# An edge-attention stage with its order taken from the source: two steps per chunk, mixing of two tiles at a time, floor and subtraction fused

## The chip, the core and the metric

The kernel runs on one core of one Trainium2 chip. The metric is device time of one execution in microseconds; the time of a kernel is the median of several executions. Engines are named as in the profile: PE (TensorE, with PEld for its weight loads), DVE (VectorE), ACT (ScalarE), POOL (GpSimd) and SP (SyncE). POOL issues the indirect DMAs that gather rows by index, and SP most other DMAs.

## What is computed

Input are 3125 nodes with 512 features and 53,125 edges (25,000 drawn pairs in both directions, and a loop at each node). Cut to its core the reference is

```python
xn = layernorm(x)
# GNN, two layers, 8 heads of 64
h = xn
for l in range(2):
    q, k, v = (h @ Wq[l].T + bq[l]) * 64**-0.5, h @ Wk[l].T, h @ Wv[l].T
    scores = einsum('ehd,ehd->eh', q[tgt], k[srcidx])          # one per edge and head
    p = exp(scores - segment_max(scores, tgt)[tgt])
    w = p / (segment_sum(p, tgt)[tgt] + 1e-16)
    attn = segment_sum(w[:, :, None] * v[srcidx], tgt) @ Wo[l].T + bo[l]
    h = batchnorm(h + attn)
    h = batchnorm(h + relu(h @ W1[l].T + b1[l]) @ W2[l].T + b2[l])
# mixing: linear attention over all nodes
qm, km = softmax(xn @ Wq.T + bq, by head), softmax(xn @ Wk.T + bk, by head)
ctx = km.T @ (xn @ Wv.T + bv)
mix = ((qm @ ctx) / (qm . sum(km)) + qm) @ Wp.T + bp
x = x + layernorm(h) + mix
x = x + mixture_of_8_experts(layernorm(x), top 2)
```

## The kernel before

Nodes are sorted by their number of edges and cut into 25 tiles of 128 (the last has 53). A tile has a fixed number of *slots* (`CAPS`: 44 for tile 0, then 26 down to 10, 453 in all): slot j holds the j-th source node of each of the 128 targets, with a mask where there is none. So one slot of one tile is one gather of 128 rows, each with V and K of a source node (4 KB), from the table `kvd` in HBM.

The program runs in stages: a front stage (layernorm, sorting, keys and values of layer 0), then for each of the two layers the *edge stage* `attention`, then feed-forward and batch norms and, between the layers, the next keys and values; at the end the experts (`last`). The change is in the edge stage.

**Blocks and chunks.** A tile is one block of slots, tile 0 two halves of 22. A block is cut into *chunks* of two slots, 232 per layer. For a chunk, `Block.scores` issues two gathers on POOL (L583), then on DVE the product of K with the query (L588) and its sum by head (L589, the *reduction*). When all scores of a block are there, `Block.exponentials` adds the mask, takes the maximum by head (L600), raises it to a floor of -1e20 (L601), subtracts it (L602) and takes the exponential on ACT (L603). `Block.weights` sums (L611) and divides. While the chunks of the next block are scored, those of this block are weighed: `weigh` multiplies V with the weights, three chunks of five by 16 activations on ACT (L624), the others on DVE (L627). `add_up` then has PE transpose and add the rows up in PSUM (L644, for half blocks L639). `finish` (L678) copies the sum, and after each group of four tiles takes the output projection in four steps: PE into the PSUM tile `po` (L701), DVE adds it to `xg` (L705).

**Lanes and places.** The gathered rows live in lanes, five in layer 0 and four in layer 1. A lane has 5 or 6 places that overlap by half: place p takes V at half p and K at half p+1, so the V of the next place of a lane overwrites the K of this one. Chunks take lanes in turn. So a gather waits for the reduction of the chunk that had the lane before (five chunks back in layer 0, four in layer 1), and, a whole round later, for the add of the chunk 20 back.

**Beside the chunks.** Generators deliver steps of other work, spread evenly over the chunks: in layer 0 `contexts` (5 steps a tile: projections of the transposed normed rows zT, exponentials, PE into the contexts), in layer 1 `mixed` (9 steps a tile, one tile at a time): projection into `pq` (L720, L723), maximum by head on DVE (`hm`, L731), exponentials on ACT (L734), reciprocal (`hr`, L740) and product on DVE (L814), transposes on PE (L454) and a copy on ACT, PE with the contexts (`mpo`, L821), reciprocal and product on DVE (`den`, L829, L830), transposes (L839), a copy, the last projection, a copy and a store. `turned` (L752) loads zT for the next tile on SP.

`places(t)` (L529) prepares tile t: in layer 0 POOL gathers its z rows into the single buffer `part` (L541), PE transposes them (L454) and ACT copies them to `xg`; in layer 1 SP loads `xg`. `query` (L551) makes the tile's q on PE (L555, L557) and ACT (L560).

**What sets the order.** The source gives the instructions in the order of this loop, and a scheduler that works on the whole edge stage decides in which order each engine takes them. Each engine takes its own in that order, and waits at the head of its queue for what an instruction needs.

Of the kernel before, what the change touches and what calls it, by code (L numbers as in the profile page):

```python
# [68 lines left out]

LAYER_COLS = 29  # L70
# [14 lines left out]
def gps_layer(ctx: ExitStack, tc: tile.TileContext, x, src, dst, cols, rows,  # L85
# [21 lines left out]
    kvd = [tc.dram_tile([N, 2 * D], F32, name=f"kvd{l}") for l in range(L)]  # L107
    wqo = [const.tile([128, NP, D], F32, name=name) for name in ("wq", "wo")]
# [280 lines left out]
    with tc.If(flag < 1) as fits:  # L389
        listed_layers(tc, cols=cols, rec=rec, idx=idx, mask=mask, kvd=kvd, zd=zd, ztd=ztd, xb=xb,  # L390
                      base=base, wqo=wqo, layer_weights=layer_weights, **args)
# [18 lines left out]
def listed_layers(ctx: ExitStack, tc: tile.TileContext, rows,  # L410
# [3 lines left out]
                  wqo, layer_weights):  # L414
# [10 lines left out]

    mixb = main.tile([128, L, NP], F32, name="mixb")
    for i, r in enumerate((ROW_BK, ROW_BQ)):
        nc.sync.dma_start(mixb[:, i, :], rows[r].rearrange("(c p) -> p c", p=128))
# [71 lines left out]
    def attention(l, stats, wq, wo, mixw):  # L500
        with tc.tile_pool(name="att", bufs=1, reuse_waits="tile") as ap, \
# [4 lines left out]
            taken_places = [0]  # L506

# [16 lines left out]

            c0 = l * LAYER_COLS + BQ
            bq = bias_rows("bq", colt[:, c0:c0 + NP])
            bm = bias_rows("bm", mixb[:, l, :])

            def places(t):  # L529
# [9 lines left out]
                if not l:  # L539
                    z = ap.tile([P, D], F32, name="part")  # L540
                    nc.gpsimd.indirect_dma_start(  # L541
                        out=z[:n], out_offset=None, in_=zd[:, :],
                        in_offset=bass.IndirectOffsetOnAxis(ap=node(t), axis=0))
                    o = (t - t0) * P
                    to_features(pp, "tr", xg[gi][:, :, o:o + n], z, n, nc.scalar.copy)
# [5 lines left out]
            def query(t):  # L551
# [8 lines left out]
                nc.scalar.activation(q[:n], ps[:n], AF.Copy, scale=float(DH) ** -0.5)  # L560
                return q

            class Block:
# [9 lines left out]
                def scores(self, i):  # L573
# [7 lines left out]
                    for k in range(g):  # L581
# [6 lines left out]
                    nc.vector.tensor_mul(ks, ks, self.q[:n, None, :].to_broadcast([n, g, D]))  # L588
                    nc.vector.tensor_reduce(  # L589
                        self.sc[:n, :, j:j + g].rearrange("p h g -> p g h"),  # L590
                        ks.rearrange("p g (h d) -> p g h d", h=H), AX.X, OP.add)

                def exponentials(self):

                    n, w = self.n, self.w
                    sc = self.sc[:n, :, :w]
                    o = OFFS[self.t] + self.j0
                    nc.vector.tensor_add(sc, sc, mask[:n, None, o:o + w].to_broadcast([n, H, w]))
                    m = ap.tile([P, H], F32, name="m", bufs=3)
                    nc.vector.tensor_reduce(m[:n], sc, AX.X, OP.max)  # L600
                    nc.vector.tensor_scalar(m[:n], m[:n], FLOOR, None, op0=OP.max)  # L601
                    nc.vector.tensor_sub(sc, sc, m[:n, :, None].to_broadcast([n, H, w]))  # L602
                    nc.scalar.activation(sc, sc, AF.Exp)  # L603
                    self.m = m

                def weights(self):

                    n, w = self.n, self.w
                    sc = self.sc[:n, :, :w]
                    s = ap.tile([P, H], F32, name="s", bufs=3)  # L610
                    nc.vector.tensor_reduce(s[:n], sc, AX.X, OP.add)  # L611
                    if self.whole:
                        inverse_sum(s, n)
                        nc.vector.tensor_mul(sc, sc, s[:n, :, None].to_broadcast([n, H, w]))  # L614
                    self.s = s
# [33 lines left out]
            def scaled(o, agg, f, n):  # L649
                for h in range(H):  # L650
                    hs = slice(h * DH, (h + 1) * DH)
                    nc.scalar.activation(o[:n, hs], agg[:n, hs], AF.Copy, scale=f[:n, h:h + 1])

# [4 lines left out]
            def together(a, b, o):  # L658
# [13 lines left out]
                part = ap.tile([P, D], F32, name="part")  # L672
                for k, e, to in ((a, f[0], o), (b, f[1], part)):
                    nc.vector.tensor_mul(e[:n], e[:n], m[:n])
                    scaled(to, k.agg, e, n)
                nc.vector.tensor_add(o[:n], o[:n], part[:n])

            def finish(blocks):  # L678
# [10 lines left out]
                else:  # L689
                    a = ap.tile([P, D], F32, name="a")  # L690
                    together(blocks[0], blocks[1], a)
                    to_features(pp, "tr", at, a, n, nc.scalar.copy)
# [65 lines left out]
            def contexts(t):  # L758

                n = TILES[t][1]  # L760
                if t + 1 < FT:
                    turned(t + 1)
                z = zT.pop(t)
# [5 lines left out]
                ps = project(n, lambda c: z[:, c, :n], wv)  # L769
                yield  # L770
# [14 lines left out]
                elif t == FT // 2:  # L785
                    rowv.append(ap.tile([P, D], F32, name="a"))
# [14 lines left out]
            def mixed(t):  # L801

                n = TILES[t][1]
                if t + 1 < FT:
                    turned(t + 1)
                z = zT.pop(t)
                ps = project(n, lambda c: z[:, c, :n], wmq, bm)
                yield
                q = ap.tile([P, D], F32, name="mq")
                s = exponentials(q, ps, n)  # L810
# [4 lines left out]
                yield  # L815
                qT = ap.tile([128, NP, P], F32, name="mqT")
                to_features(pp, "tr", qT[:, :, :n], q, n, nc.scalar.copy)
# [17 lines left out]
                oT = ap.tile([128, NP, P], F32, name="mqT")  # L835
# [7 lines left out]
                nc.scalar.copy(oT[:, :, :n], ps[:, :NP * n].rearrange("p (c r) -> p c r", c=NP))  # L843
# [3 lines left out]
                y = ap.tile([P, D], F32, name="my")  # L847
# [4 lines left out]
            def beside():  # L852
                for t in range(FT):
                    yield from mixed(t) if l else contexts(t)
# [10 lines left out]
            each = 9 if l else 5  # L865
            steps, done, taken = beside(), 0, 0
            number = FT * each
            chunks = sum((w + G - 1) // G for t, j0, w in todo if t < FT - 2)
            chunks += (todo[0][2] + G - 1) // G

            before, held, ending = None, [], iter(())
            places(0)
            turned(0)
            q = query(0)
            places(1)
            for _ in range(each):
                next(steps)
                taken += 1
            for t, j0, w in todo + [(None, 0, 0)]:
                now, k = None, 0  # L880
                if t is not None:
                    now = Block(t, j0, w, q)
                    k = len(now.chunks)
                kb = len(before.chunks) if before else 0
                for i in range(max(k, kb)):
                    if i < k:
                        now.scores(i)
                        done += 1 if before else 2
                    if i == 0 and before:
                        before.weights()  # L890
                    if i < kb:
                        before.weigh(i)
                    next(ending, None)
                    while (taken - each) * chunks < (number - each) * done and taken < number:
                        next(steps)
                        taken += 1
                    if i < kb:
                        before.add_up(i)
# [825 lines left out]
```

## Time and profile before

| | |
|---|---|
| median of 3 runs | 2837.37 us (2830.23 to 2837.75) |
| the profiled execution | 2804.75 us |
| its span, first to last instruction | 2803.0 us |
| mean granted PE clock | 0.911 |
| edge stage of layer 0, first product to the last output projection | 284 to 1103 us |
| edge stage of layer 1 | 1347 to 2266 us |
| gathers L583 | 906, 1.27 us each on POOL, median 6.3 us from issue to landing |
| products L588 | 464, 1.19 us each on DVE |
| reductions L589 | 464, 1.19 us each on DVE |
| weighing on ACT, L624 | 3888 activations of 0.34 us |
| weighing on DVE, L627 | 214, 1.20 us each |

How to read the lines that follow below. A line of the timeline has start, duration, engine, line of the kernel, operation, output <- inputs, form, count, and in brackets the idle time before it with what the profile thinks ended it. A row of a group has busy time and mean ns of one after the bar. A row of waits names the waiting instruction, the one waited for, then the total in us, the number of waits and the longest. Of several things waited for, the profile names the one whose event came last, and this is inferred.

### The profile page before, as it was taken

To read this page: it belongs to the slowest core of one execution; us is meant where nothing else is said; L and a number is where in the kernel's file an instruction comes from. 1 tells how busy PE (TensorE), PEld (TensorE's weight loads), DVE (VectorE), ACT (ScalarE), POOL (GpSimd) and SP (SyncE) were. 2 spreads that over 40 slices of the span, in tenths; PEclk is the share of its full clock that TensorE was granted. 3 is DMA by queue.
4 is the path that set the end of the run, shared out by engine and by line. 5 is a ranking of instruction groups with operands and counts; after the bars stand their busy time and mean duration, and the time that the engine had idled before them with its cause. 6 is when DMAs were issued, how large, how long until landed. Compare 5 with 4: busy or idle time off the path is not lost. (4 is left out here: it accounts for less than half of the span.)

```text
span 2803.0 us, 30800 instructions
## 1 busy us (share of the span) xinstructions
PE 2398.1 (86%) x8935; PEld 1302.4 (46%) x8935; DVE 2054.1 (73%) x3186; ACT 1406.5 (50%) x5315; POOL 1414.4 (50%) x1153
## 2 busy tenths in 40 slices
PE   6987989889889876999697787979888486999998
PEld 3442445545455543344344555555555344444443
DVE  7810999999999985500679888989988566666663
ACT  1111568787776763200276767776767423222220
POOL 3362778888777770011657766676765323222100
PEclk9998999999999987999798888989999796999999
DMA  8434999999999984321869888989887441111000
GB/s 287 171 121 138 328 331 337 332 330 338 330 326 325 332 266 159 122 108 78 286 234 335 287 299 292 329 303 331 309 307 269 131 135 51 34 48 48 32 19 20
DMA packets 214478, 620.58 MB, mean 221 GB/s; under 512 B 48068, under 2 KB 53569, under 8 KB 210199
## 3 DMA queue, kind: packets, MB, share of 16 engines
q0 software_dynamic: 161696, 518.18, 52.4%
q1 hardware_dynamic: 50048, 95.36, 9.4%
q10 hardware_dynamic: 2556, 4.97, 0.5%
q8 instruction: 75, 1.23, 0.2%
q14 instruction: 103, 0.84, 0.1%
HBM read 543.80 MB, written 74.75 MB: 221 GB/s over the span
## 5 line engine op out<-in xcount | busy, mean ns | idle before, releaser
L583 POOL DMA_INDIRECT lane<-kvd,idx x906 | 1147.7, 1267 | 526.7 <-issue 179.7
L624 ACT ACTIVATE lane<-lane,sc 128x64 f32<-128x64 f32 x3888 | 945.4, 339 | 117.9 <-DVE sc L614 117.6
L588 DVE TENSOR_TENSOR lane<-lane,q 128x1024 f32<-128x1024 f32 (+1 forms) x464 | 549.0, 1193 | 161.8 <-DMA lane<-kvd,idx 146.7
L644 PE MATMUL agg<-ident,lane 128*128 128x128 f32 (+1 forms) x3272 | 531.6, 301 | 140.5 <-DVE lane L627 59.5
L644 PEld LDWEIGHTS agg<-ident,lane 128*128 128x128 f32 (+1 forms) x3272 | 424.2, 154 | 316.1 <-ACT lane L624 143.5
L589 DVE TENSOR_REDUCE sc<-lane 128x16 f32<-128x1024 f32 (+1 forms) x464 | 545.5, 1187 | 2.6 <-ACT lane L624 1.6
L627 DVE TENSOR_TENSOR lane<-lane,sc 128x1024 f32<-128x1024 f32 (+1 forms) x214 | 252.3, 1197 | 0.1
L1089 DVE SCALAR_TENSOR_TENSOR yall<-py,prob,yall 128x512 f32<-128x512 f32 (+1 forms) x200 | 148.8, 748 | 112.4 <-PE py L1087 100.8
L555 PE MATMUL pq<-wq,xg 128*128 128x512 f32 (+1 forms) x400 | 201.7, 634 | 18.5 <-ACT kt L734 12.2
L701 PE MATMUL po<-aT,wo 128*128 128x512 f32 (+1 forms) x448 | 194.2, 572 | 20.3 <-ACT aT L688 13.4
L1087 PE MATMUL py<-w2t,hT 128*128 128x512 f32 (+1 forms) x400 | 188.7, 610 | 1.8 <-ACT hT L1083 0.8
L1080 PE MATMUL ph<-xT,w1t 128*128 128x512 f32 x320 | 156.3, 630 | 0.0
L1095 POOL DMA_INDIRECT out<-yall,rec x25 | 25.0, 1001 | 252.3 <-DVE yall L1089 247.4
L1083 ACT ACTIVATE hT<-ph,colt 128x512 f32<-128x512 f32 (+1 forms) x56 | 35.4, 633 | 211.0 <-PE ph L1080 210.8
L494 POOL DMA_INDIRECT kvd<-kv,rec x25 | 24.7, 989 | 222.8 <-DVE kv L491 216.8
L491 DVE COPY kv<-pv 128x512 f32<-128x512 f32 (+1 forms) x25 | 17.3, 692 | 153.4 <-PE pv L488 153.4
L701 PEld LDWEIGHTS po<-aT,wo 128*128 128x128 f32 x448 | 80.3, 202 | 97.9 <-issue 64.9
L1087 PEld LDWEIGHTS py<-w2t,hT 128*128 128x128 f32 (+1 forms) x400 | 71.9, 189 | 101.3 <-issue 69.0
L555 PEld LDWEIGHTS pq<-wq,xg 128*128 128x128 f32 (+1 forms) x400 | 73.4, 199 | 92.8 <-issue 68.3
L372 ACT COPY kv<-pkv 128x512 f32<-128x512 f32 (+1 forms) x50 | 29.2, 585 | 163.8 <-PE pkv L370 136.4
L1012 POOL DMA_INDIRECT bt<-base,rec x25 | 26.8, 1072 | 160.1 <-DVE yall L1019 150.3
L370 PE MATMUL pkv<-wk,xT 128*128 128x512 f32 (+1 forms) x200 | 100.7, 637 | 5.8 <-ACT kv L372 5.8
(264 smaller groups left out, 3288.4 us busy)
## 6 DMA issues: line engine op xcount, KB each, us to landing
lane<-kvd,idx POOLq DMA_INDIRECT x906, 6.3
kvd<-kv SPq DMA_DIRECT2D x24, 512.0 KB, 2.7
zT<-ztd SPq DMA_DIRECT2D x48, 256.0 KB, 5.3
xmid<-xg SPq DMA_DIRECT2D x10, 1024.0 KB, 5.7
xT<-xmid POOLq DMA_DIRECT2D x10, 1024.0 KB, 10.3
xr<-in_x SPq DMA_DIRECT2D x24, 256.0 KB, 3.9
xb<-xo SPq DMA_DIRECT2D x24, 256.0 KB, 5.6
zd<-z SPq DMA_DIRECT2D x24, 256.0 KB, 2.7
```

The lines of the kernel that those rows point to most:

```text
L370: nc.tensor.matmul(ps[:n], lhsT=xT[t][:, c, :n], rhs=wkv[name][:, c, :], start=(c == 0), stop=(c == NP - 1))
L555: nc.tensor.matmul(ps[:n], lhsT=of_place(t, c), rhs=wq[:, c, :], start=(c == 0), stop=False)
L583: gets.append(nc.gpsimd.indirect_dma_start(out=kv[:n, k, :], out_offset=None, in_=kvd[l][:, :], in_offset=bass.IndirectOffsetOnAxis(ap=idx ...
L588: nc.vector.tensor_mul(ks, ks, self.q[:n, None, :].to_broadcast([n, g, D]))
L589: nc.vector.tensor_reduce(self.sc[:n, :, j:j + g].rearrange("p h g -> p g h"), ks.rearrange("p g (h d) -> p g h d", h=H), AX.X, OP.add)
L624: nc.scalar.activation(v[:, k, h, :], v[:, k, h, :], AF.Copy, scale=self.sc[:n, h, j + k:j + k + 1])
L627: nc.vector.tensor_mul(v, v, self.sc[:n, :, j:j + g].rearrange("p h g -> p g h")[:, :, :, None] .to_broadcast([n, g, H, DH]))
L644: nc.tensor.matmul(self.agg[:, c * n:(c + 1) * n], lhsT=kv[:n, k, c * 128:(c + 1) * 128], rhs=ident[:n, :n], is_transpose=True, start=firs ...
L701: nc.tensor.matmul(ps[:, :w], lhsT=wo[:, kk, c * 128:(c + 1) * 128], rhs=aT[gi][:, kk, :w], start=(kk == 0), stop=(kk == NP - 1))
L1080: nc.tensor.matmul(ph[:, :w], lhsT=w1t[:, e, c, :], rhs=xT[:, c, gs], start=(c == 0), stop=(c == NP - 1))
L1087: nc.tensor.matmul(py[:n], lhsT=hT[:, i * P:i * P + n], rhs=w2t[:, e, :], start=True, stop=True)
L1089: nc.vector.scalar_tensor_tensor(yall[:n, t, :], py[:n], prob[:n, i, e:e + 1], yall[:n, t, :], op0=OP.mult, op1=OP.add)
```

## The change

The loop of the edge stage and its preparation stand inside `tc.manual_schedule` for PE, DVE, ACT, POOL and SP: these five take their instructions in the order of the source. The source is written anew for this:

- `scores` is split. `products(i)` issues the gathers and the product of chunk i; the reduction of chunk i-1 comes after it.
- `exponentials`, `masked`, `summed` and `weights` are separate, so that the mask is added at the end of a block, maximum, subtraction and exponential come after the first product of the next block, sum and weights after its second.
- `later` holds work that is issued one step later: copies of the transposes, the query's copy, adds, and the end of a block.
- `places` is split into `fetch(t+2)`, issued at the third chunk of tile t, and `turn_fetched(t+1)` at its second chunk.
- The floor goes into the subtraction, as one `scalar_tensor_tensor` (max with FLOOR, then minus the scores), with `scale=-1` in the exponential; the two half blocks keep the separate floor.
- The two halves of tile 0 are put together by DVE (eight operations that multiply and add) where ACT scaled the second half into `part` and DVE added.
- `mixed` has 12 steps, and two tiles are in work at once, six steps apart; `mq` has two buffers. At the start one step of `contexts` is issued ahead where it was five, and six of `mixed` where it was nine.
- The load of `mixb` moves from SP, inside the branch, to ACT's queue ahead of the front stage. `turned(t+1)` is issued later within the tile. The row buffers `a` and `my` become `rowv` and `mo`.

```diff
+            def fetch(t):
...
                 if not l:
-                    z = ap.tile([P, D], F32, name="part")
+                    fetched[t] = ap.tile([P, D], F32, name="part")
                     nc.gpsimd.indirect_dma_start(
-                        out=z[:n], out_offset=None, in_=zd[:, :],
+                        out=fetched[t][:n], out_offset=None, in_=zd[:, :],
                         in_offset=bass.IndirectOffsetOnAxis(ap=node(t), axis=0))
-                    o = (t - t0) * P
-                    to_features(pp, "tr", xg[gi][:, :, o:o + n], z, n, nc.scalar.copy)
+
+            def turn_fetched(t):
+                if t in fetched:
+                    n, o = TILES[t][1], t % GT * P
+                    ps = turned_over(fetched.pop(t), n)
+                    later.append(lambda: nc.scalar.copy(xg[t // GT][:, :, o:o + n], by_chunk(ps, n)))
...
+                    m = self.m = ap.tile([P, H], F32, name="m", bufs=3)
+                    nc.vector.tensor_reduce(m[:n], sc, AX.X, OP.max)
+                    if not self.whole:
+                        nc.vector.tensor_scalar(m[:n], m[:n], FLOOR, None, op0=OP.max)
+                    nc.vector.scalar_tensor_tensor(sc, m[:n, :, None].to_broadcast([n, H, w]), FLOOR, sc,
+                                                   op0=OP.max, op1=OP.subtract)
+                    nc.scalar.activation(sc, sc, AF.Exp, scale=-1.0)
...
+                for t in range(FT + 1):
+                    now = mixed(t) if t < FT else iter(())
+                    for _ in range(6):
+                        next(ahead, None)
+                        next(now, None)
+                        yield
+                    ahead = now
...
+            with tc.manual_schedule(engines=ORDERED):
...
+                    for i in range(max(k, kb)):
+
+                        if i < k:
+                            now.products(i)
+                            done += 1 if before else 2
+                        if i == 0 and before:
+                            before.exponentials()
+                        if i == 1 and before:
+                            before.summed()
+                        if 0 < i < k:
+                            now.scores(i - 1)
+                        if i == 1 and before:
+                            before.weights()
+                            before.weigh(0)
+                        if 0 < i < kb:
+                            before.weigh(i)
+                        if i == k - 1:
+                            now.scores(i)
+                            now.masked()
+                        next(ending[0], None)
+                        run_later()
+                        while (taken - ahead) * chunks < (number - ahead) * done and taken < number:
+                            next(steps)
+                            taken += 1
+                        if i == 1 and before:
+                            later.append(lambda b=before: b.add_up(0))
+                        if 0 < i < kb:
+                            later.append(lambda b=before, i=i: b.add_up(i))
+                        if i == kb - 1:
+                            later.append(lambda b=before: summed(b))
+                        if now and j0 + w == CAPS[t]:
+                            if i == 1 and t + 1 < FT:
+                                turn_fetched(t + 1)
+                            if i == 2 and t + 2 < FT:
+                                fetch(t + 2)
+                            if i == max(k - 4, 2) and t + 1 < FT:
+                                q = query(t + 1)
```

## The prediction

> **What bounds the kernel now.** I read the engines' shares first, then their busy time by stage, then what the bounding engine waits for in each edge stage, and last the timeline around those waits. The shares name PE:
>
> ```profile
> PE 2398.1 (86%) x8935; PEld 1302.4 (46%) x8935; DVE 2054.1 (73%) x3186; ACT 1406.5 (50%) x5315; POOL 1414.4 (50%) x1153
> ```
>
> That is an average over the whole program. The change touches only the two edge stages, which I bound by their first product and the last tile's output projection. The columns are length, then PE, PEld, DVE, ACT and POOL with busy time and instructions, the granted PE clock, the DMA share, GB/s. The first two rows are the middles of layers 0 and 1, the last two the whole stages.
>
> ```profile
> core 0: us, PE busy (x) PEld busy (x) DVE busy (x) ACT busy (x) POOL busy (x), PEclk, DMA share, GB/s
> 330.00:1012.00 682.00, 606.05 (x2508) 344.17 (x2507) 643.33 (x808) 522.02 (x2223) 541.83 (x420) 0.94 0.91 326
> 1440.00:2170.00 730.00, 612.91 (x2647) 379.72 (x2645) 641.84 (x844) 520.81 (x2164) 471.56 (x379) 0.90 0.84 299
> 284.00:1103.00 819.00, 702.47 (x2889) 400.18 (x2889) 747.11 (x958) 578.28 (x2463) 603.85 (x471) 0.93 0.88 314
> 1347.00:2266.00 919.00, 737.68 (x3084) 450.11 (x3084) 768.33 (x1018) 606.17 (x2513) 571.86 (x461) 0.88 0.82 288
> ```
>
> DVE sets the pace of both: 747 of 819 us in layer 0, 768 of 919 in layer 1, so 72 and 151 us idle. In the middle of layer 0 it is 94% busy with the DMA engines at 91%: little is to be had there. Layer 1 has the room, at 88% and 84%. What ended DVE's idle time, layer 1 first, then the largest row of layer 0:
>
> ```profile
> DVE lane L588 <- DMA lane<-kvd,idx: 97.5, 54, 11.2
> DVE xg L705 <- PE po L701: 19.8, 10, 4.1
> DVE hm L731 <- PE pq L723: 19.0, 5, 10.0
> DVE den L829 <- PE mpo L821: 9.3, 10, 1.8
> DVE hr L740 <- ACT mq L734: 4.2, 3, 2.5
> ...
> DVE lane L588 <- DMA lane<-kvd,idx: 49.2, 43, 5.1
> ```
>
> Of layer 1's 151 us, 97.5 are products that wait for a gather and 32.5 are the mixing's three handoffs (hm, den, hr). Why are the gathers late? POOL's waits there blame PE's adds:
>
> ```profile
> POOL lane L583 <- PE agg L644: 73.3, 64, 11.2
> POOL lane L583 <- DVE sc L589: 33.0, 38, 5.0
> POOL lane L583 <- PE agg L639: 23.6, 7, 21.0
> ```
>
> I don't believe the name. The adds meant (20 chunks back) ended 10 to 40 us earlier. Matching each gather to the instruction that it needs, I find the layer-1 gathers starting 0.3 to 0.7 us after the end of the reduction four chunks back, whose K half they overwrite:
>
> ```profile
> 1454.10 1.19 DVE L589 TENSOR_REDUCE sc<-lane 128x16 f32<-128x1024 f32 x1
> ...
> 1456.04 2.67 POOL L583 DMA_INDIRECT lane<-kvd,idx  x1 [20.99 <-PE agg L639]
> ```
>
> The reduction ends at 1455.29, the gather starts at 1456.04, and POOL had stood 21 us. So it is a loop: reduction, gather, product. DVE was itself late here because of a mixing step 10 us before, which is how one late handoff of the mixing comes back as a gather wait:
>
> ```profile
> 1443.37 0.69 DVE L731 TENSOR_REDUCE hm<-pq 128x8 f32<-128x512 f32 x1 [9.99 <-PE pq L723]
> ```
>
> **Part by part.** The sum is made against the profiled execution, 2804.75 us (span 2803.0); the median of the runs, 2837.37, lies 32.6 us above it, and I carry the difference over unchanged.
>
> *The order.* Nothing of a chunk's own work goes: 906 gathers, a product (1.19 us) and a reduction (1.19) for each of 464 chunks, the same weighing. The reduction now stands one chunk after its product, so PE, ACT and POOL get more notice, but a place comes free one product later. I summed the durations of the DVE work that stands between the reduction which frees a place and the product which needs it. Median in layer 1: 10.2 us before, 8.2 after; in layer 0, whose places lie five chunks apart: 13.8, then 11.2. Against it stands the time from the end of a reduction to the landing of the second gather it frees: median 8.2 us over 96 chunks of layer 1, deciles 7.1 and 9.6 (0.3 to start, some 1.5 for the first gather's turn on POOL, 6.3 from issue to landing). With 8.2, 112 of 224 chunks of layer 1 come short, by 158 us in all. One wait also serves the chunks that share its loop, three of them, so 158/3 = 53 us. With 7.1 it is 52/3 = 17, with 9.6 it is 350/3 = 117. In layer 0 the same sum gives 0 to 26/4, about 1.
>
> Here a rule speaks for a much larger gain. The Trainium skill, "DMA: Bandwidth & Descriptors", section "Anatomy of one DMA — SWDGE (gpsimd) path", gives a DMA 2.0 us and its bytes over 436 GB/s: 524,288 bytes come to 3.2 us. The loop would close in 0.3 + 1.5 + 3.2 + 2.3 (product and reduction) = 7.3 us for three chunks, 2.4 each, below DVE's 768/232 = 3.31 a chunk, and no place would ever be waited for: 53 us less. The row has 6.3, with three to four gathers in flight at once sharing the engines; then it is 10.5 us, 3.5 each, just above 3.31. I take the row.
>
> Layer 1's gather waits: 53, and 7 for the first landing, which nothing covers in either kernel, so 60 for 97.5: -37.5.
>
> *Mixing, two tiles at once, 12 steps.* The instructions are the same; each handoff gets a step between the engines. Hm gets 8.4 us of DVE work as cover where it had 6.8 (lower quartile), den 7.0 for 3.4, hr about 4.6 for 3.4. PE needs 2 to 4 us for each when its queue is clear; the exponentials take 4.2 us on ACT. I put hm at 2 us (layer 0's row for it has 2.1), den at 4, hr at 6: 12 for 32.5, -20.5. Low 0; high the present 32.5, if PE's queue holds projections behind adds which wait for ACT.
>
> *Output projection.* Four times PE, then DVE, with a single bank of PSUM as before; 19.8 and 15.8 us remain. Draining what is left of it before a new block costs 4 us in layer 1 and 2 in layer 0, where the next tile has eight chunks or fewer.
>
> *Floor.* 48 of 52 blocks lose the op (row L601: 171 ns): 8 us of DVE, 4 a layer. The subtraction (298 ns) becomes a scalar_tensor_tensor. The Trainium skill, "Vector Engine (DVE) Microarchitecture Reference", section "7. Points that are easy to get wrong", says that this form with two sources in SBUF that aren't bf16 halves throughput, which would add up to 52 × 0.15 = 8 us and eat the saving. The trace has such a form:
>
> ```profile
> L1017 DVE SCALAR_TENSOR_TENSOR yall<-yall,mv,gt 128x512 f32<-128x512 f32 x24 | 18.5, 772 | 0.1
> ```
>
> A TENSOR_TENSOR of that size takes 684 ns (L773), so 13% more: 52 × 0.04 = 2 us. Tile 0's two halves trade eight activations and an addition (0.69 us) for eight small DVE operations (about 0.2 each, from the smallest rows): +1 a layer. Net: -2 a layer. None of this is hidden, since DVE is the bound.
>
> *The z rows of layer 0.* This is the danger. The gather of z for tile t+2 stands, in POOL's order, ahead of the gathers of chunk 3 of tile t. Its one buffer is read by PE's transposes of tile t+1, which stand behind the adds of the last tile's first chunks, which wait for ACT's weighing. Whoever waits there holds every later edge gather. Before, the scheduler placed these; all idle time before L541 was 11.2 us. After the transposes it takes 0.6 + 1.25 (z's own turn) + 1.5 + 6.3 = 9.7 us until chunk 3 has landed, with one to two chunk times of 3.36 us ahead of DVE and what had already landed. Bounds over 23 tiles: 0, and a whole latency each, 6.3 × 23 = 145. I take 1.65 each, 38 us, nearer the low end, since two or three chunks have usually landed ahead. With 1 for places and 5 for scattered waits that is 44 for 49.2: -5. The head adds 5: the z gather of tile 1 now waits for tile 0's transposes, ahead of chunk 0's gathers (3 to 6 by the rows).
>
> *At nothing.* The bias rows' load, moved to ACT's queue ahead of the branch, lies under the front stage. The later loads of zT have a tile of time (34 us) against 5.3 us. ACT has 26 us of work in a 34-us tile, so deferred copies find room; uncovered they would cost 0.6 us each. PE issues 24 instructions more, ten us at most, with 76 idle in layer 0's middle.
>
> Sum: layer 1 -37.5 - 20.5 + 4 - 2 = -56; layer 0 -5 + 5 + 2 - 2 = 0, and 1 for both stages' last deferred steps: -55. 2804.75 - 55 = 2750; on the median **2782 us**.
>
> **Rivals.** *Places never bind, z never holds:* landing by 7.1 us takes 53 to 17, and a clear POOL takes some more off the 38: -55 - 36 - 4 = -95, about 2742; with z at 0, 2715 and below. For: deferral evens out DVE, and 7.1 is only a decile away. Against: the 91% DMA share.
>
> *Places bind harder:* at 9.6 us, 117 for 53, so +64: 2846. For: two gathers now start back to back as soon as a reduction ends. Against: nine of ten landings were quicker.
>
> *The z gather holds POOL (the slower side):* with a hold of h per tile the sum is -55 - 38 + 23h, so it decides from h = 4.0 us. At the whole latency, 6.3, it is +52: 2889. For: the strict order and PE at 89% in layer 0's middle. Against: the waits of before on that line were small.
>
> *It does not do what it says:* DVE and DMA are nearly full, and each wait removed returns as another: 2837.
>
> **How the numbers follow.** The forecast 0.44 (its own range 2757 to 2812), no binding 0.15, harder binding 0.10 (0.04 of it within the bound), the z hold 0.27, no effect 0.04. About 0.3%, 8.5 us, is what a measurement here can tell from no change: faster 0.59, same 0.08, slower 0.33. The range 2715 to 2880 takes in z holds up to 5.9 us and nearly all of the fast side.
>
> **What would show it.** Layer 1's row "lane from kvd" at 60 us and hm, den and hr together near 12: right; at 120 or more, places bind. POOL's idle time before the z gathers of 1 to 2 us a tile: right; 4 or more: the rival. A floor row with four instructions in all, DVE 8 to 12 us less over the two stages. Layer 1's stage should shrink to about 863 us, layer 0's stay within 20 of 819. I'm wrong if the stages swap roles, or if PE, with its queue in order, waits for ACT so long that adds delay DVE.

## The result, and the profile after

The changed kernel takes 3057.74 us (median of 4, 3053.17 to 3059.98) where the kernel before took 2833.8 in the same set: a ratio of 1.079 (95% interval 1.076 to 1.081), 224 us slower. The forecast was 2782 us, 55 faster. The profiled execution has 3056.15 us and a span of 3054.4.

The shares of the page have not turned round; every engine has more idle time:

```profile
PE 2504.3 (82%) x8935; PEld 1335.9 (44%) x8935; DVE 2096.1 (69%) x3152; ACT 1401.0 (46%) x5299; POOL 1403.3 (46%) x1153
```

The same windows as before, from each layer's first product to its last output projection (columns: length, then PE, PEld, DVE, ACT and POOL, PE clock, DMA share, GB/s):

```profile
299.00:1273.00 974.00, 754.88 (x2883) 427.48 (x2881) 764.26 (x938) 576.67 (x2454) 600.16 (x475) 0.87 0.76 266
1522.00:2515.00 993.00, 785.61 (x3084) 453.69 (x3084) 784.14 (x994) 599.49 (x2489) 561.49 (x455) 0.85 0.78 264
```

Layer 0, which was to stay at 819 us, has 974; layer 1, which was to shrink from 919 to 863, has 993. These are 155 and 74 us of the 251 by which the profiled span grew; 15 lie ahead of the first product, 5 between the layers and 2 behind them. DVE's busy time rose by 17 and 16 us, its idle time from 72 to 210 and from 151 to 209. From the last product to the last output projection it takes 38 us in each layer, where it took 35 and 32. What DVE waited for, layer 0 and then layer 1:

```profile
DVE lane L617 <- DMA lane<-kvd,idx: 160.5, 73, 23.5
DVE xg L745 <- PE po L741: 45.1, 18, 7.1
...
DVE vt L813 <- PE pq L760: 5.2, 4, 2.5
```

```profile
DVE lane L617 <- DMA lane<-kvd,idx: 107.5, 73, 10.1
DVE xg L745 <- PE po L741: 50.8, 21, 7.2
DVE mo L873 <- DMA base<-mo: 8.1, 2, 4.4
DVE hm L771 <- PE pq L763: 7.8, 3, 4.3
...
DVE hr L780 <- ACT mq L774: 5.4, 8, 2.5
```

Before, the rows for gathers and for `po` were 49.2 and 15.8, then 97.5 and 19.8. (The 23.5 us in layer 0's first row is the wait that ends with its first product, outside the stage.) Two things come out: gathers are late in layer 0, and DVE now waits 96 us for the output projection where it waited 36.

Why the gathers are late in layer 0 stands in POOL's waits there. The gather of the z rows (L553) is held in 21 waits, 154 us, about 6.7 us for each of 23 tiles:

```profile
POOL part L553 <- PE tr L567: 80.2, 14, 12.7
POOL part L553 <- PE agg L684: 42.3, 4, 13.0
...
POOL part L553 <- DVE s L691: 20.4, 1, 20.4
```

One such tile, from the timeline. PE's transposes start at 603.68; the z gather, which POOL has had at the head of its queue for 9.62 us, starts as they end; the edge gathers follow it, and DVE's next product stands 6.32 us for their landing:

```profile
603.68 0.66 PE L567 MATMUL tr<-ident,part 128*128 128x128 f32 x4
...
604.60 0.97 POOL L553 DMA_INDIRECT part<-zd,rec  x1 [9.62 <-PE agg L684]
...
613.32 1.23 DVE L617 TENSOR_TENSOR lane<-lane,q 128x1024 f32<-128x1024 f32 x1 [6.32 <-DMA lane<-kvd,idx]
```

Why the output projection is late stands in PE's waits in layer 0, before and after:

```profile
PE agg L644 <- DVE lane L627: 23.1, 8, 10.7
...
PE agg L644 <- ACT lane L624: 3.3, 12, 0.7
...
PE po L701 <- ACT aT L688: 2.6, 3, 1.2
```

```profile
PE agg L684 <- DVE lane L667: 93.8, 34, 9.7
PE agg L684 <- ACT lane L664: 33.6, 35, 7.8
PE po L741 <- ACT aT L727: 28.7, 6, 6.9
```

PE now stands at adds whose chunk isn't weighed, and at the output projection until ACT has copied the sum, while in its fixed order nothing may pass. Its idle time in layer 0 went from 116 to 219 us, the gaps longer than 3 us from 8 to 27. In layer 1 the wait for DVE's weighing went from 36.4 to 82.1 us and that for the copy from 10.8 to 27.5, but PE's whole idle time only from 180 to 207, since other waits fell. The end of one group shows what follows:

```profile
1128.38 6.24 PE L741 MATMUL po<-aT,wo 128*128 128x512 f32 x8 [6.90 <-ACT aT L727]
...
1145.01 3.70 PE L741 MATMUL po<-aT,wo 128*128 128x512 f32 x8
...
1148.75 0.75 DVE L745 SCALAR_TENSOR_TENSOR xg<-po,colt,xg 128x512 f32<-128x512 f32 x1 [6.96 <-PE po L741]
```

PE stood 6.90 us, took 6.24 us for eight matmuls that take 3.70 a little later, and had adds, a projection and a query ahead of the next output projection in its order; it worked without a break, and DVE stood 6.96 us for the result.

### The profile page after: what moved, and what is told of

It reads as the page before. It is cut to its first block, busy times and chain, and to the rows that moved or that the text cites. A ratio compares the mean times of both kernels' runs of the same rounds, so it can differ in the third digit from the quotient of the medians.

```text
span 3054.4 us, 30739 instructions
## 1 busy us (share of the span) xinstructions
PE 2504.3 (82%) x8935; PEld 1335.9 (44%) x8935; DVE 2096.1 (69%) x3152; ACT 1401.0 (46%) x5299; POOL 1403.3 (46%) x1153
## 5 line engine op out<-in xcount | busy, mean ns | idle before, releaser
L612 POOL DMA_INDIRECT lane<-kvd,idx x906 | 1134.7, 1252 | 564.2 <-issue 265.3
L684 PE MATMUL agg<-ident,lane 128*128 128x128 f32 (+1 forms) x3272 | 563.3, 310 | 299.1 <-DVE lane L667 175.9
L741 PE MATMUL po<-aT,wo 128*128 128x512 f32 (+1 forms) x448 | 212.5, 624 | 63.8 <-ACT aT L727 56.1
L582 PE MATMUL pq<-wq,xg 128*128 128x512 f32 (+1 forms) x400 | 195.5, 635 | 1.3 <-ACT xg L561 1.3
L741 PEld LDWEIGHTS po<-aT,wo 128*128 128x128 f32 x448 | 88.5, 218 | 159.2 <-issue 89.1
L553 POOL DMA_INDIRECT part<-zd,rec x25 | 30.7, 1229 | 224.9 <-PE tr L567 135.4
L760 PE MATMUL pq<-wmp,mqT 128*128 128x512 f32 (+1 forms) x200 | 109.9, 701 | 15.7 <-ACT mqT L887 15.6
L587 ACT ACTIVATE q<-pq 128x512 f32<-128x512 f32 (+1 forms) x50 | 29.9, 599 | 181.3 <-PE pq L584 171.9
```

The lines of the kernel that those rows point to most:

```text
L582: nc.tensor.matmul(ps[:n], lhsT=of_place(t, c), rhs=wq[:, c, :], start=(c == 0), stop=False)
L612: gets.append(nc.gpsimd.indirect_dma_start(out=kv[:n, k, :], out_offset=None, in_=kvd[l][:, :], in_offset=bass.IndirectOffsetOnAxis(ap=idx ...
L684: nc.tensor.matmul(self.agg[:, c * n:(c + 1) * n], lhsT=kv[:n, k, c * 128:(c + 1) * 128], rhs=ident[:n, :n], is_transpose=True, start=firs ...
L741: nc.tensor.matmul(ps[:, :w], lhsT=wo[:, kk, c * 128:(c + 1) * 128], rhs=aT[gi][:, kk, :w], start=(kk == 0), stop=(kk == NP - 1))
L760: nc.tensor.matmul(ps[:n], lhsT=lhs(c), rhs=w[:, c, :], start=(c == 0), stop=(c == NP - 1 and bias is None))
```

## The experiments

The kernel before took 2798 to 2834 us in the different sets of runs, so each kernel is given by its ratio to the kernel before in its own set; the changed kernel's is 1.079. A *point* is 1% of the kernel before, some 28 us. Where stages are compared, lengths are from the profiled executions, to about 1 us, and are not set off against the kernel before of the same set: layer 0 of e2, which that edit leaves alone, has 966 us where the changed kernel has 974. Differences of that size say nothing.

**The whole order.** In e4 the changed source is kept and the fixed order is dropped:

```diff
-            with tc.manual_schedule(engines=ORDERED):
+            with ExitStack():
```

> The changed kernel's source, with no fixed order: the scheduler orders all engines as in the kernel before. Theory A and B (the order costs, not the instructions): 2810 to 2850, level with the kernel before or a little under it, since 48 small DVE operations are gone and mixing has two tiles in work. Rival C (the new source itself costs, by its later reductions and adds and its z gathers' place): 2900 or more, since the scheduler goes by the source's order where nothing else decides.

Measured: 1.0037 (1.002 to 1.005). The windows of e4, layers 0 and 1, are those of the kernel before again:

```profile
277.00:1096.00 819.00, 711.80 (x2888) 402.21 (x2886) 748.21 (x937) 575.23 (x2454) 611.53 (x473) 0.93 0.89 316
1340.00:2254.00 914.00, 748.38 (x3078) 435.44 (x3076) 764.88 (x998) 600.52 (x2505) 570.80 (x459) 0.89 0.84 289
```

So 7.5 of the 7.9 points are the fixed order. The rival that the new source costs by itself is out as a sum, 0.4 points; parts of it cost and gain under the scheduler, as shown at the end of this section.

**Which engine's order.** Each of these takes one engine or more out of the set `ORDERED`, for instance

```diff
-ORDERED = {mybir.EngineType.PE,
-           mybir.EngineType.DVE,
+ORDERED = {mybir.EngineType.DVE,
```

> The changed kernel, with POOL's order left to the scheduler and the other four engines in the order of the source. Theory A: the z gathers no longer hold the edge gathers, so layer 0 gives back 60 to 110 us, layer 1 nothing: 2950 to 2995. Rival B (PE's and DVE's order hold everything, POOL only follows): within 20 us of the changed kernel, 3038 to 3078.

> The changed kernel with PE's order left to the scheduler, DVE, ACT, POOL and SP in the order of the source. Of the 7.9% over the kernel before, the run with no fixed order gave back 7.5%. Theory P (PE stands at adds whose chunk isn't weighed yet, with the z transposes, projections and output projections behind them): ratio to the kernel before 1.02 to 1.045, the waits of xg for po and of the z gathers for PE fall by half. Theory D (DVE's own order costs): 1.065 or more.

> The changed kernel with DVE's order left to the scheduler, the other four in the order of the source. Theory D (DVE stands at single operations of the mixing and the output projection that are not ready, while products or reductions further back are): ratio 1.02 to 1.045, xg's waits (94 us in both layers) fall below 40. Theory P: 1.065 or more, since z gathers and places are as late as before.

> The changed kernel with ACT's order left to the scheduler, the other four in the order of the source. Theory A (ACT's copies for the output projection and the exponentials stand behind chunks of 16 activations, 3.9 us each): ratio 1.05 to 1.065. Theories P and D: 1.07 to 1.08, ACT only follows.

> The changed kernel with PE's and ACT's order left to the scheduler; DVE, POOL and SP in the order of the source. Freed alone, PE gave back 4.3% of the 7.9% and ACT 2.6%. Theory S (one loss: PE stands for ACT's weighing and ACT's copies for PE, so that freeing both gives little more than freeing PE): ratio 1.025 to 1.035. Theory T (two losses that add up): ratio 1.00 to 1.015, POOL's order is then worth 1% at most.

> The changed kernel with only DVE and SP in the order of the source. With PE and ACT free it stood at 1.022, with all free at 1.004. If POOL's order was the rest: 1.003 to 1.010. If DVE's order (late reductions, additions of the output projection at a fixed place) is: 1.015 to 1.022.

| order left to the scheduler | ratio | 95% interval | layer 0, layer 1 (us) |
|---|---|---|---|
| none (the changed kernel) | 1.079 | 1.076 to 1.081 | 974, 993 |
| POOL (e3) | 1.059 | 1.055 to 1.064 | 905, 991 |
| PE (e5) | 1.036 | 1.031 to 1.040 | 882, 965 |
| DVE (e6) | 1.089 | 1.084 to 1.094 | 988, 1024 |
| ACT (e7) | 1.052 | 1.049 to 1.056 | 928, 951 |
| PE and ACT (e9) | 1.022 | 1.020 to 1.023 | 844, 947 |
| PE, ACT and POOL (f4) | 1.036 | 1.033 to 1.038 | 849, 965 |
| all (e4) | 1.004 | 1.002 to 1.005 | 819, 914 |

Freed alone, PE's order gives back most (4.3 points), ACT's and POOL's follow (2.6 and 2.0, with intervals that overlap). These three came out in the range of their theories P, A and A. Freeing DVE's order alone, against theory D, makes things worse: POOL's standing at the z gathers (shown below for the changed kernel, 154 us) becomes 220 us. PE and ACT freed together give 5.7 points, which lies between theories S and T: less than the 6.9 of both alone, more than PE's 4.3, so the two losses overlap in part. With them free PE's wait for DVE's weighing in layer 0 is 28.8 us, where it was 93.8 in the changed kernel and 23.1 before, and the clock is back at 0.91:

```profile
PE agg L682 <- DVE lane L665: 28.8, 22, 4.2
```

In layer 1 that wait stays at 86.5 us, and the stage at 947 where it was 919 before.

Freeing POOL as well lost 1.4 points again (f4), against both expectations. The loss is in layer 1, where the products' waits for gathers rise from 114 to 137 us. With these three free, what remains fixed is DVE's order and SP's, and it costs 3.2 points (f4 against e4), though DVE's cost nothing when it was freed first; SP's was never freed alone. The effects don't add up, and a partly free order is not between its ends.

**The z gather.** In e1 it is issued at the tile's last chunk where it was at the third:

```diff
-                            if i == 2 and t + 2 < FT:
+                            if i == k - 1 and t + 2 < FT:
                                 fetch(t + 2)
```

> The changed kernel, with the gather of the z rows for tile t+2 issued at the last chunk of tile t where it was at the third; no other instruction moves. Theory A (in layer 0 POOL stands at the z gather until PE has transposed the rows before, and every edge gather behind it comes late): POOL's idle time before the z gathers falls from 154 us in layer 0 to under 40, the products' waits for gathers there from 160 us to 50 to 70, and the kernel by 80 to 110 us, to about 2950 to 2980. Rival B (the fixed order as such: whichever engine is late holds the others, and one wait removed comes back as another): less than 30 us, 3030 or more.

Measured: 1.064 (1.060 to 1.068), 1.45 points or 41 us less. POOL's hold before the z gathers fell from 154 us to 7, layer 0 from 974 to 920 us. DVE's waits there:

```profile
DVE lane L617 <- DMA lane<-kvd,idx: 80.5, 44, 22.9
DVE xg L745 <- PE po L741: 65.5, 23, 7.3
DVE vt L813 <- PE pq L760: 14.0, 9, 3.5
```

The products' waits fell by more than half (22.9 of the 80.5 end with the first product, outside the stage), but xg's rose from 45 to 66 and vt's from 5 to 14, both waits for PE. So the hold is real and both theories have a part: of 154 us of POOL's standing, 41 came back, between the 80 of theory A and the 30 of rival B.

**Reductions of layer 1.** In e2 they follow their products at once (`if l: now.scores(i)` behind `now.products(i)`, and the later call kept for layer 0).

> The changed kernel, with layer 1's reductions taken straight after their products, as before the change; layer 0 is untouched. Theory A (in layer 1 the gathers wait for the reduction four chunks back, which comes one product later than before): POOL's waits for reductions in layer 1 fall from 288 us towards 140, the products' waits for gathers from 107 us to 50 to 70, and the kernel by 35 to 55 us, to 3000 to 3020. Rival B: DVE now waits elsewhere (den, hm, xg), and the kernel falls by less than 15 us, 3043 or more.

Measured: 1.075 (1.071 to 1.079), 0.35 points or 10 us, which is not clear of the noise: the interval overlaps the changed kernel's. In the profiled execution layer 1 went from 993 to 967 us. Its largest waits:

```profile
DVE xg L745 <- PE po L741: 49.1, 18, 7.7
DVE sc L622 <- ACT lane L664: 37.5, 12, 7.4
DVE lane L617 <- DMA lane<-kvd,idx: 14.5, 7, 7.0
```

The gather waits fell from 107 to 14.5, far below what I expected, and a new row of 37.5 us came: reductions that wait for ACT. By the source the score buffer has two copies, and ACT's weighing of the block before the last reads the one that the new block's first reduction writes; no run tests this reading. So theory A was right about the gathers and rival B about the time: giving the place back earlier took the gather waits away, and DVE waited elsewhere.

**Four moves within the fixed order.** e8 moves DVE's addition of the output projection to the end of its step, e11 issues adds and the end of a block one step later (`later.append(lambda: later.append(...))`), f1 calls `run_later()` at the start of the step, so that ACT's copies come ahead of the step's weighing and PE's adds ahead of the step's output projection, and g1 puts one more `yield` ahead of a group's first output projection.

> The changed kernel with DVE's addition of the output projection and its statistics moved from the start to the end of the same step; everything else keeps its place. If xg's waits (43 us in layer 0, 50 in layer 1, 32 of them in the tails of the stages) come from DVE taking the addition too early in its order, those outside the tails fall from 62 us to 20 or less and the ratio from 1.079 to about 1.06 to 1.068. If the time only moves on to the next gathers, the ratio stays at 1.073 or more.

> The changed kernel, fixed order, with PE's adds of a chunk (and the end of a block) issued one step later still. If PE loses its time standing at adds whose chunk isn't weighed yet (176 us for DVE's weighing, 47 for ACT's over both layers), these waits fall below 100 us in sum and the ratio from 1.079 to 1.045 to 1.065. If PE only stands there because DVE is late for another reason, its waits move to other lines and the ratio stays at 1.072 to 1.082.

> The changed kernel, fixed order, with the postponed work of a step (ACT's copies of transposes, queries and sums, PE's adds) issued at the start of the next step, ahead of that step's 16 activations of weighing, where it came behind them. Theory C (PE stands at the output projection for ACT's copy of the sum, L727, and at the query's successors, because the copies stand behind chunks of 3.9 us): PE's 56 us of waits for that copy fall below 20, xg's waits from 94 to under 65, the ratio from 1.079 to 1.050 to 1.065. Rival (the copies wait for PE's last adds, not for ACT's turn): 1.070 or more.

> The changed kernel, fixed order, with the output projection of a group starting one step later after ACT's copy of the last sum. Theory: PE's waits for that copy (56 us in both layers) fall below 25 us, PE's granted clock in layer 0 rises above 0.87, xg's waits fall from 94 us to 60 to 75, ratio 1.060 to 1.072. Rival: short tiles drain the group at their end, so that the step is lost again, or PE waits elsewhere: 1.075 or more.

Measured: e8 1.075 (1.072 to 1.078), e11 1.074 (1.072 to 1.076), f1 1.086 (1.083 to 1.088), g1 1.072 (1.069 to 1.075). The interval of e8 overlaps the changed kernel's too. Only g1's ratio is in the range of its theory, and just so; e8, e11 and f1 are in those of their rivals. In e8 xg's waits stayed at 46 and 50 us: where in the step DVE takes the addition isn't it. In f1 PE's waits for the copy fell as theory C had it, over the whole program, first the changed kernel and then f1:

```profile
PE po L741 <- ACT aT L727: 56.1, 12, 6.9
```

```profile
PE po L741 <- ACT aT L727: 11.4, 9, 4.2
```

So the rival's reason, that the copies wait for PE's last adds, is out, though the rival's number came. (PE's adds now standing ahead of the projection may have part in the fall; in e7, where they do not move and ACT's order is free, these waits are 3.8 us.) The time was lost elsewhere: POOL stood 180 us at the z gathers of layer 0 where it had been 154, and ACT 253 us over the program for PE's queries (L587) where it had been 172. In g1 PE's wait for the copy is gone from its list, xg's waits fell from 94 to 78 (waits above 0.3 us in the two stages), and PE's wait for DVE's weighing grew in layer 0:

```profile
PE agg L684 <- DVE lane L667: 101.1, 43, 9.7
```

So it is worth 0.7 points at most, the clock stayed at 0.87, and xg's waits missed the 60 to 75 of the theory. In e11 later adds were to take these waits away. Those for DVE's and ACT's weighing fell from 223 to 168 us over both layers, not below 100, and others came in layer 0:

```profile
PE agg L684 <- DVE lane L667: 84.2, 36, 15.2
PE po L741 <- ACT aT L727: 38.7, 7, 10.4
PE ctxp L818 <- DVE vt L815: 29.1, 12, 6.6
```

**Do the repairs add up?** g2 has e1, e2 and e8 in one kernel, f2 has f1 and e1.

> The changed kernel, fixed order, with the z gather at the last chunk of the tile, layer 1's reductions straight after their products, and DVE's additions of the output projection at the end of the step. Alone they gave 1.45, 0.35 and 0.4 points. Separate losses: 1.053 to 1.061. One loss seen in three places: 1.062 to 1.068. If removing one wait lets the next gain count in full: below 1.05.

> The same with the z gather at the last chunk of the tile. If the two causes are separate: the gain of the first plus 1.45 points, 1.035 to 1.05. If they are one (the z transposes were late because PE was): the better of the two, 1.05 to 1.064.

g2: 1.057 (1.054 to 1.060), 2.2 points, just the sum of the three alone, though two of these three are within the noise by themselves. f2: 1.063 (1.060 to 1.065), like e1 by itself and in the range of one cause; f1's loss and e1's gain added up would be 1.071. So what f1 lost is gone once the z gather is moved, which fits the longer standing at the z gathers that f1 showed. No kernel in which all five orders are fixed came below 1.057.

**Parts of the change under the scheduler.** e10 is e4 with reductions at once in both layers; e12 is the kernel before with the fused floor alone; f3 adds mixing of two tiles in 12 steps to e12.

```diff
-                    nc.vector.tensor_scalar(m[:n], m[:n], FLOOR, None, op0=OP.max)
-                    nc.vector.tensor_sub(sc, sc, m[:n, :, None].to_broadcast([n, H, w]))
-                    nc.scalar.activation(sc, sc, AF.Exp)
+                    if not self.whole:
+                        nc.vector.tensor_scalar(m[:n], m[:n], FLOOR, None, op0=OP.max)
+                    nc.vector.scalar_tensor_tensor(sc, m[:n, :, None].to_broadcast([n, H, w]), FLOOR, sc,
+                                                   op0=OP.max, op1=OP.subtract)
+                    nc.scalar.activation(sc, sc, AF.Exp, scale=-1.0)
```

> The changed kernel's source with all orders left to the scheduler, and each reduction straight after its product in both layers. Against the scheduler's run with later reductions (ratio 1.004; 163 us of POOL's waits in layer 1 bound by a reduction, 63 us of DVE's on those): if the later reduction costs places under the scheduler too, DVE's waits for gathers in layer 1 fall from 121 us to 60 to 100 and the ratio to 0.985 to 0.998, below the kernel before. If the scheduler had already evened this out: 1.000 to 1.006.

> The kernel before with the floor fused into the subtraction alone (halves of tile 0 keep the separate floor). By the rows: 48 operations of 171 ns go, 8.2 us, and the fused form costs 6 ns more than the subtraction in 52 blocks, 0.3 us: ratio 0.996 to 0.998. If the form halved DVE's rate: 48 x 0.171 less 52 x 0.15, level: 1.000. If the scheduler places other work differently: anything within 0.5%.

> The kernel before, all orders by the scheduler, with the fused floor and with mixing of two tiles at once in 12 steps; nothing else of the change. The fused floor alone stood at 0.989. If two tiles at once take away the 18 us of hm's waits in layer 1 and nothing else moves: 0.982 to 0.988. If the gathers are what ends last and take it back: 0.987 to 0.993. If the fused floor's gain beyond its 8 us was an accident of the scheduler's order: 0.992 or more.

Measured: e10 0.993 (0.992 to 0.994), e12 0.989 (0.988 to 0.991), f3 0.985 (0.983 to 0.987). e10 and f3 came as their first theories had them, e12 outside all its ranges. Later reductions cost 1.1 points under the scheduler (e4 against e10; the row of gather waits in layer 1 is 108.0 us, then 92.9). The fused floor gained 1.1 points, 30 us, where its operations are worth 8; part of the rest is fewer gather waits (49 to 28 us in layer 0), and why they fell is not shown: the scheduler's order on all engines differs as well. That the gain stands in f3 speaks against an accident, no more. Two tiles at once did what it was for: layer 1 of f3 is 17 us shorter than e12's 903, and the 18 us of hm's waits are gone from its list.

```profile
1327.00:2213.00 886.00, 747.51 (x3079) 431.10 (x3077) 761.08 (x989) 602.85 (x2513) 558.23 (x459) 0.89 0.85 298
```

f3 is the fastest kernel here, 2757.46 us beside 2800.25 for the kernel before in its set.

## Why the prediction was wrong, point by point

*What bounds it* was right: DVE sets the pace, PE's share of busy time misleads, and in layer 1 gathers wait for the reduction four chunks back. First gathers of a chunk that started within 0.9 us of that reduction's end, after a wait, make up some 290 us of POOL's idle time there, where it was some 145.

*The step that failed* is in "The order" and "At nothing". I gave PE, ACT and POOL "more notice" and wrote "PE issues 24 instructions more, ten us at most, with 76 idle in layer 0's middle". That idle time is only cover if other work may move into it. In a fixed order it may not: PE's idle time in layer 0 rose from 116 to 219 us, and is 168 with PE's order free, 128 with ACT's as well, and 107 with all of them. The instructions themselves weren't it: the page counts 8935 on PE in both kernels. DVE's waits for `po`, which I let "remain" at 19.8 and 15.8 with 6 for draining, became 50.8 and 45.1. I named this in the last sentence, and under the z rival as "PE at 89%", but gave it neither a sum nor a chance of its own. It is the largest term that a run shows: 5.7 of 7.9 points with ACT's. Part of the z hold below is in it, since with PE's order free POOL stands 56 us at the z gathers and not 154.

*The z gather* was the named rival, and its mechanism was right; the size I took for the forecast, 1.65 us a tile, was not. I counted chunks that had landed ahead as cover, but POOL stood 6.7 us a tile, and in the tile shown above DVE stood 6.32 us behind it. That passes the point of decision (4.0 us); taken at its full length, the sum for this rival gives 61 us over the kernel before, 116 over the forecast. Not all of that was there to be had: moving the z gather gave back 41 (e1).

*Places in layer 1*: I forecast 53 us. Of the products' waits in layer 1, about 78 us stood on gathers that had waited for the reduction. The latency was right: where DVE waited for such a gather, from the reduction's end to the product took a median of 8.3 us (8.2 forecast). What was off is the division by three, my guess of how far one wait serves the chunks behind it: 158 us over 78 is two. And by e2, taking these waits away is worth some 10 us of the kernel, within the noise.

*Mixing*: hm 7.8, hr 5.4 and den 7.5 us (4.0 for `mpo`, 3.5 in two smaller rows) make 21 for the 12 forecast, where it was 32.5; new are 8.1 us for the store out of the shared buffer `mo`, which I had passed over. The saving was right in kind (f3), and swamped here.

*Floor*: right by its operations. The fused form takes 304 ns where the subtraction took 298, so the Trainium skill's rule that it halves throughput, named in the prediction, is not seen here; my 13% from the larger form was still too much. For both stages' last deferred steps I had put 1 us; the ends of the stages grew by 3 and 6.

*The head* grew by 15 us in the profiled execution, where 5 were forecast; in the experiments with a fixed order the first product came at 276 to 306 us, so I rest nothing on it.

*Small slips in the working*: with 6.3 us to landing the loop is 10.4 us, where I wrote 10.5; the rival with no z hold at all sums to 2708, where I wrote 2715; and the gather in the lines I showed starts 0.75 us after its reduction, not within 0.3 to 0.7. None of them moves the forecast.

*What stays open*: which pairs in PE's and ACT's orders make the 5.7 points. Copies ahead of the weighing take away the waits for them, but not the time; later adds and an added step are small. Least is known of layer 1's 74 us: the one move made there alone (e2) is within the noise. Also open are why gathers come later in layer 1 when POOL is freed beside PE and ACT, why DVE's and SP's orders cost 3.2 points once the others are free, and the fused floor's other 22 us.

## What to carry to other kernels

An engine's idle time covers later or slower work only where something may be put into it: before fixing the order of a heavily loaded engine, ask of each of its waits who stands behind it. An engine that runs ahead of the others, as POOL does with gathers, loses its lead at an instruction that waits for an engine that runs behind; here that was 1.45 points. And try the parts of a rewriting under the old order: here two of them gained 1.5%, most of it not explained, hidden under an order that cost 7.5.

## What the runs showed of the hardware

PE's clock fell with its standing. From before to after the granted clock went from 0.93 to 0.87 in layer 0 and from 0.88 to 0.85 in layer 1, and PE's busy time for the same matmuls rose by 52 and 48 us; without the fixed order (e4) the clock was 0.93 and 0.89 again.

The clock records of the traces know two values, full and half. In layer 0 there were 19 stretches at half before, with 86 us of PE's work in them, and 39 after, with 192 us. Half of that work time is lost, 43 and 96 us: 53 more, which is the whole rise. In layer 1 it is 24 stretches with 134 us of work, then 37 with 206: 36 of the 48 us; what the other 12 are is not shown. The group's end above is one of them: the clock is at half from 1126.7 to 1133.5 us, after PE's 6.90 us of standing, and 5.15 of the 6.24 us of the eight matmuls lie in it.

The Trainium skill, "TensorE: Matmul & The Clock Gate", section "Part 1: The HAM clock gate (the "warmup" mystery)", has PE at half clock after an idle window of about 3.4 us, until about as long a busy stretch. The traces agree in the unit: in both stages every stretch at half is 3.41 us or a whole multiple of it, 6.9 us on average in layer 0 after. By that rule 19 more gaps over 3 us in layer 0 would cost an estimated 19 x 3.4 / 2 = 32 us of PE, and 5 more in layer 1 an estimated 9; the clock records give 53 and 36, so counting long gaps underrates it. An engine with 14% of idle time on the page lost part of that room through the way in which it was idle. How much of the 224 us this made by itself no run tells apart.
